# Moving the layernorms' normalized results from VectorE to ScalarE in a fused tokenizer, retention and MoE kernel

## The chip, the cores and the metric

The kernel runs on one NeuronCore of a Trainium2 chip. The metric is device time in microseconds (us) from the first to the last instruction of one execution; lower is better. The engines are called by their profile names: PE (TensorE matmul) and PEld (its weight load), DVE (VectorE), ACT (ScalarE), POOL (GpSimd) and SP (SyncE, which issues most of the DMA transfers). Each engine works through its own list of instructions, and semaphores join the lists.

## What is computed

The reference, cut to its steps, with D = 256 features, H = 1024, 8 experts, and 4 x 64 rows of 64 tokens (16,384 tokens):

```python
h = tok_ref(x, W)                          # patches -> rfft -> 256 features
# attention-like block on the layernorm of h
z  = layernorm(h)
zz = layernorm(z) * ln1_g + ln1_b
q, k, v = zz @ Wq.T + bq, zz @ Wk.T + bk, zz @ Wv.T + bv
mem_t = decay * mem_{t-1} + k_t * v_t ;  ret_t = q_t * mem_t
z  = z + ret
zz = layernorm(z) * ln2_g + ln2_b
h  = h + z + relu(zz @ W1.T + b1) @ W2.T + b2
# mixture of experts on the layernorm of h, the best 2 of 8 experts
tok = layernorm(h)
h   = h + tok + sum_over_2_experts(share_e * (gelu(tok @ w1[e] + b1[e]) @ w2[e] + b2[e]))
```

So each token passes four layernorms. The first two are one after the other (z, then zz from the same h: its factor is worked out directly from the variance of h), the third is zz after the retention, and the fourth is tok before the experts. Gains and offsets of the layernorms are folded into the weights; what is left of each is (x - mean) * rstd.

## The kernel before: the parts that matter

The tokens are worked on in 32 blocks of 512 (4 groups of 128 tokens, TT = 4). Three blocks are under way at a time: `new` is embedded and goes through retention, `mid` goes through the MLP, `old` is routed to the experts. Between them "slots" run expert tiles of 256 rows. The order on PE, DVE, ACT and SP is the order of the program text. Cuts are marked with `...`; line numbers of the profile (L252) are those of the whole kernel.

```python
    p_mm = ctx.enter_context(tc.tile_pool(name="p_mm", bufs=4, space=...PSUM))   # 4 buffers
    p_tm = ctx.enter_context(tc.tile_pool(name="p_tm", bufs=3, space=...PSUM))
    ...
        def factors(self, twice=False):            # on GpSimd: rstd = (var + eps) ^ -0.5
            ...
            nc.gpsimd.tensor_tensor(self.rstd, self.rstd, mhalf[:, 0:n, :], ALU.pow)    # L248

        def apply(self, dst, src, i=0):            # L252: (x - mean) * rstd, on DVE
            for t in range(TT):
                nc.vector.tensor_scalar(dst[:, t, :D], src[:, t, :], self.mv[:, t, 0:1],
                                        self.rstd[:, i, t : t + 1], ALU.subtract, ALU.mult)
    ...
    class Turn:                                    # a transpose of 32-bit data by DMA, as two 16-bit planes
        def split(self, src):                      # L278: two ACT copies  planes <- src
            ...
        def start(self, planes):                   # L286: SP issues DMA transposes  turned <- planes
            ...
        def join(self, dst, copy):                 # L292: four copies  dst <- turned
            ...
    def feature_mm(w, rhs, m):                     # L298
        ps = p_mm.tile([P, BLK], F32, name="mm")
        for k in range(KD):
            nc.tensor.matmul(ps, lhsT=w[:, k, ts(m, P)], rhs=rhs[:, k, :], ...)
        return ps
    ...
        def embed(self):
            ... # products of x on PE, sums on DVE, statistics of h on DVE
            norm.factors(twice=True)
            yield
            self.z = one.tile(...); self.zz = one.tile(...)
            norm.apply(self.zz, self.h, 1)
            norm.apply(self.z, self.h, 0)
        ...
        def residual(self):
            ... # ret transposed by PE (L451), z += ret (L454), statistics of z, on DVE
            norm.factors_here()                    # 12 small DVE instructions, L231 to L237
            self.zz = one.tile([P, TT, D], F32, name="zz")
            norm.apply(self.zz, self.z)
        ...
        def features2(self):                       # ACT copies hT <- turned
            self.turn.join(self.hT, nc.scalar.copy)

        def mlp_in(self, m):                       # m = 0..7
            ps = feature_mm(w1_sb, self.hT, m)
            nc.scalar.activation(self.aT[:, m, :], ps, AF.Relu, ...)                    # L482

        def mlp_out(self, u, ...):                 # L492 on PE, h += ps on DVE (L499), statistics
            ...
            if u == U - 1:
                self.norm.factors_here() if self.i >= NS - 1 else self.norm.factors()
                self.tok = one.tile([P, TT, D], F32, name="tok")
                self.norm.apply(self.tok, self.h)
                ...
                nc.vector.tensor_scalar(self.by[:, 0, :], rstd, 1.0, None, ALU.add)
                nc.vector.scalar_tensor_tensor(self.by[:, 1, :], mean, -1.0, rstd, ALU.mult, ALU.mult)

        def store(self):                           # L518: h = h * by0 + by1, four ACT instructions
            ...
            self.stored = nc.sync.dma_start(out=rows_of(self.i), in_=self.h)

        def rows(self):                            # L533: row <- tok, two ACT copies
            ...
    ...
    class Tile:                                    # 256 rows of one expert
        def turn(self):    ...                     # L792: xT <- xh, two ACT copies
        def enter(self):   ...                     # L799: ps = p_mm.tile(...), matmuls; L807: ge <- gelu(ps), ACT
        def leave(self):   ...                     # L816: ps = p_tm.tile(...), matmuls
        def sums(self):    ...                     # y on DVE, added to the output by an indirect DMA of GpSimd
    ...
            # one block of the loop
            embed = new.embed()
            next(embed)
            if mid: mid.features2()
            if old:
                old.rows()
                old.turn3()
                old.store()
            next(embed)
            next(embed)
            if mid: mid.sum_up()
            next(embed, None)
            slot(known)                            # an expert tile: turn of the next but one, enter, leave
            if old: old.join3()
            ...
            for m in range(KH):
                if mid: mid.mlp_in(m)
                if m == 1: new.split1()
                if m == TT - 1: slot(known)
                if m == KH - 3:
                    blocks[i + 1].differences(xs.pop(i + 1))
                    new.features1()
            ...     # logits of old, retention of new, slot, mid.mlp_out(0)
            new.residual()
            slot(known)
            ...
            new.split2()
            if mid: mid.mlp_out(1)
```

Of the kernel before, what the change touches and what calls it, by code (L numbers as in the profile page):

```python
# [12 lines left out]
F32 = mybir.dt.float32  # L13
# [6 lines left out]
P = 128  # L20
# [15 lines left out]
def vit_tower_kernel(  # L36
# [178 lines left out]
    class Norm:  # L215
# [23 lines left out]
        def factors(self, twice=False):  # L239
# [7 lines left out]
                )  # L247
            nc.gpsimd.tensor_tensor(self.rstd, self.rstd, mhalf[:, 0:n, :], ALU.pow)  # L248

        def apply(self, dst, src, i=0):  # L250
            for t in range(TT):
                nc.vector.tensor_scalar(  # L252
                    dst[:, t, :D],
                    src[:, t, :],
                    self.mv[:, t, 0:1],
                    self.rstd[:, i, t : t + 1],
                    ALU.subtract,
                    ALU.mult,
                )
# [49 lines left out]
    class Block:  # L309
# [32 lines left out]
        def embed(self):  # L342


            xv = self.xv.rearrange("p i (j w) n -> p i j (w n)", j=J)
            self.h = three.tile([P, TT, D], F32, name="h")
            h = [self.h[:, t, :] for t in range(TT)]

            def products(which):
                ps = p_tm.tile([P, 2, D], F32, name="tm")  # L350
                for n, i in enumerate(which):
                    for j in range(J):
                        nc.tensor.matmul(  # L353
                            ps[:, n, :], lhsT=xv[:, i, j, :], rhs=wu[:, i, j, :], start=j == 0, stop=j == J - 1
                        )
# [24 lines left out]
            norm.stats(self.h, TT - 1)  # L380
            norm.factors(twice=True)
            yield
            self.z = one.tile([P, TT, D], F32, name="z")
            self.zz = one.tile([P, TT, D], F32, name="zz")
            norm.apply(self.zz, self.h, 1)
            norm.apply(self.z, self.h, 0)

        def split1(self):
            if self.i < EARLY:
# [55 lines left out]
        def residual(self):  # L445
            norm = Norm()
            for u in range(U):
                ps = p_tm.tile([P, 2, D], F32, name="tm")
                for i in range(2):
                    for k in range(KD):  # L450
                        nc.tensor.transpose(  # L451
                            ps[:, i, ts(k, P)], self.ret[:, k, ts(2 * u + i, P)], ident
                        )
                nc.vector.tensor_tensor(self.z[:, ts(u, 2), :], ps, self.z[:, ts(u, 2), :], ALU.add)  # L454
                for i in range(2):
                    norm.stats(self.z, 2 * u + i)
            norm.factors_here()
            self.zz = one.tile([P, TT, D], F32, name="zz")
            norm.apply(self.zz, self.z)

        def sum_up(self):
            nc.vector.tensor_tensor(self.h, self.h, self.z, ALU.add)
# [2 lines left out]
        def split2(self):  # L465
            if self.i < EARLY:
                return
            self.turn = Turn()
            self.turn.split(self.zz)

# [13 lines left out]
        def mlp_out(self, u, between=None):  # L484
            if u == 0:
                self.norm = Norm()
            ps = p_tm.tile([P, 2, D], F32, name="tm")
            for i in range(2):
                if i and between:
                    between()  # L490
                for k in range(KH):
                    nc.tensor.matmul(  # L492
                        ps[:, i, :],
                        lhsT=self.aT[:, k, ts(u * 2 + i, P)],
                        rhs=w2_sb[:, k, :],
                        start=k == 0,
                        stop=k == KH - 1,
                    )
            nc.vector.tensor_tensor(self.h[:, ts(u, 2), :], ps, self.h[:, ts(u, 2), :], ALU.add)  # L499
            for i in range(2):  # L500
                self.norm.stats(self.h, u * 2 + i)
            if u == U - 1:
                self.norm.factors_here() if self.i >= NS - 1 else self.norm.factors()
                self.tok = one.tile([P, TT, D], F32, name="tok")
                self.norm.apply(self.tok, self.h)
                if self.i == NS:
                    nc.vector.tensor_tensor(self.h, self.h, self.tok, ALU.add)
                    return
                mean, rstd = self.norm.mv[:, :, 0], self.norm.rstd[:, 0, :]
                self.by = small.tile([P, 2, TT], F32, name="by")  # L510
                nc.vector.tensor_scalar(self.by[:, 0, :], rstd, 1.0, None, ALU.add)
                nc.vector.scalar_tensor_tensor(self.by[:, 1, :], mean, -1.0, rstd, ALU.mult, ALU.mult)

        def store(self):

            by = self.by
            for t in range(TT):
                nc.scalar.activation(  # L518
                    self.h[:, t, :],
                    self.h[:, t, :],  # L520
                    AF.Identity,
                    bias=by[:, 1, t : t + 1],
                    scale=by[:, 0, t : t + 1],
                )

            self.stored = nc.sync.dma_start(out=rows_of(self.i), in_=self.h)
# [1 line left out]

        def rows(self):

            self.row = two.tile([P, TT, RW], I32, name="row")
            for i, half in enumerate(halves(self.tok)):
                nc.scalar.copy(self.row.bitcast(U16)[:, :, i * D : (i + 1) * D], half)  # L533
# [415 lines left out]
    with tc.manual_schedule(engines=MANUAL):  # L949
        blocks[0].differences(xs.pop(0))  # L950
        xs[1] = load_x(1)
        for i in range(NS):
# [12 lines left out]
                old.turn3()  # L965
                old.store()
            next(embed)
            next(embed)
            if mid:
                mid.sum_up()  # L970
            next(embed, None)
            slot(known)
            if old:
                old.join3()
# [2 lines left out]
            for m in range(KH):  # L977
                if mid:
                    mid.mlp_in(m)
                if m == 1:  # L980
                    new.split1()
                if m == TT - 1:
                    slot(known)
                if m == KH - 3:
# [35 lines left out]
        old.turn3()  # L1020
        old.store()
        next(embed)
        next(embed)
        mid.sum_up()
        next(embed, None)
        expert_step()
        weights = load_bank()
        old.join3()
        for m in range(KH):
            mid.mlp_in(m)  # L1030
            if m in (1, 5):
                next(weights)
            if m == TT - 1:
# [150 lines left out]
```

## Time and profile before

| | before |
|---|---|
| time, median of 3 runs | 2202.25 us (2193.75 to 2203.81) |
| span of the profiled execution | 2216.1 us |
| PE busy | 2161.2 us, 98% |
| DVE busy | 1650.9 us, 74% |
| POOL busy | 873.1 us, 39% |
| ACT busy | 825.6 us, 37% |
| the four results of layernorms on DVE (L252), 128 instructions each | 44.8 + 44.2 + 44.2 + 44.0 us |

A row of the profile's groups names line, engine, operation, output <- inputs and shape; then the busy time and the mean of one in ns; then the idle time of the engine just before, and what ended it. A row of the timeline gives start and duration in us, and in brackets the idle time before it with its releaser. One matmul of the program text (32-bit) stands in the profile as two records, so one step `mlp_in(m)` is four records of 128x512.

### The profile page before, as it was taken

Reading aid. Unit: us, or ns where it says so; the run is one execution under the profiler, and the core shown is the slowest. Engines: PE = TensorE matmul, PEld = TensorE weight load, DVE = VectorE, ACT = ScalarE, POOL = GpSimd, SP = SyncE. Lnnn points to the kernel's source line nnn. Section 1 sums busy time; section 2 is a strip of 40 time slices with the busy share of each in tenths; the row PEclk is TensorE's granted clock in tenths of the full one; section 3 lists DMA queues with packets and bytes.
Section 4 is the critical chain, followed back from the end, with each engine's and each line's share of the span. In section 5 each row is a group of like instructions: output and inputs, shape, how many; then the busy total and the mean of one; then the engine's idle time right before and its main releaser. Section 6 shows DMA issues by size and latency. Waiting matters only on the chain.

```text
span 2216.1 us, 28920 instructions
## 1 busy us (share of the span) xinstructions
PE 2161.2 (98%) x8548; PEld 1544.3 (70%) x8548; DVE 1650.9 (74%) x5150; ACT 825.6 (37%) x1329; POOL 873.1 (39%) x760
## 2 busy tenths in 40 slices
PE   8999999999999999999999999999999999998999
PEld 6666666667676667777666777666677766676676
DVE  6678877778778777877877777777787777766454
ACT  1223323444334443432444432344443334442443
POOL 0022243344444434444434444443444444344444
PEclk9999999999999999999999999999999999999999
DMA  3022265676565677657567656665765666588743
GB/s 135 20 97 75 79 147 125 134 163 122 127 149 135 143 139 150 125 129 155 129 139 149 135 128 135 149 136 132 163 130 130 138 146 137 115 172 205 116 66 45
DMA packets 425389, 284.95 MB, mean 129 GB/s; under 512 B 355216, under 2 KB 391056, under 8 KB 421136
## 3 DMA queue, kind: packets, MB, share of 16 engines
q1 hardware_dynamic: 374304, 210.21, 41.4%
q0 software_dynamic: 49632, 67.39, 16.1%
q10 hardware_dynamic: 1296, 5.52, 1.0%
q8 instruction: 67, 1.10, 0.2%
q14 instruction: 90, 0.74, 0.1%
HBM read 118.36 MB, written 88.39 MB: 93 GB/s over the span
## 4 chain that ended last, share of the span: by engine, by line
PE 88%; DVE 3%; DMA 3%; ACT 3%; issue 2%; another core or an unknown queue 0%; POOL 0%; ACTq 0%; DVEq 0%; SPq 0%; POOLq 0%
PE mm L298 31%; PE tm L492 19%; PE tm L353 11%; PE mm L799 9%; PE tm L816 9%; DMA turned<-planes 3%; PE sm L557 2%; PE tm L888 1%; PE tm L451 1%; PE mm L871 1%; PE mm L131 1%; PE mm L265 1%; ACT h L518 1%; ACT row L533 1%; ACT hT L292 1%
## 5 line engine op out<-in xcount | busy, mean ns | idle before, releaser
L839 POOL DMA_INDIRECT out<-y,xg x262 | 429.3, 1638 | 501.0 <-DVE y L835 225.9
L492 PE MATMUL tm<-w_sb,aT 128*128 128x256 f32 x2048 | 462.3, 380 | 16.5 <-issue 14.6
L298 PE MATMUL mm<-hT,w_sb 128*128 128x512 f32 x1024 | 455.4, 596 | 10.7 <-ACT ge L807 5.7
L492 PEld LDWEIGHTS tm<-w_sb,aT 128*128 128x128 f32 x2048 | 387.2, 190 | 80.8 <-issue 27.1
L298 PEld LDWEIGHTS mm<-hT,w_sb 128*128 128x128 f32 x1024 | 193.9, 191 | 232.6 <-issue 207.6
L298 PE MATMUL mm<-hT,wqkv_sb 128*128 128x512 f32 x768 | 342.5, 602 | 4.2 <-DVE hT L292 4.2
L640 POOL DMA_INDIRECT xbuf<-row,to x248 | 242.3, 977 | 258.8 <-DVE full L699 182.4
L807 ACT ACTIVATE ge<-mm,w 128x256 f32<-128x256 f32 x262 | 109.3, 469 | 574.3 <-issue 525.8
L353 PE MATMUL tm<-wu,xv 128*128 128x256 f32 x1280 | 284.8, 381 | 0.0
L298 PEld LDWEIGHTS mm<-hT,wqkv_sb 128*128 128x128 f32 x768 | 145.3, 192 | 176.4 <-issue 160.4
L353 PEld LDWEIGHTS tm<-wu,xv 128*128 128x128 f32 x1280 | 244.3, 191 | 33.3
L799 PE MATMUL mm<-xT,w 128*128 128x256 f32 x1048 | 251.3, 383 | 1.5 <-DVE tile_share L828 1.5
L816 PE MATMUL tm<-w,ge 128*128 128x256 f32 x1048 | 247.6, 379 | 0.9 <-DVE y L833 0.9
L482 ACT ACTIVATE aT<-mm,vec 128x512 f32<-128x512 f32 x256 | 169.9, 684 | 173.7 <-PE mm L298 170.5
L799 PEld LDWEIGHTS mm<-xT,w 128*128 128x128 f32 x1048 | 195.6, 191 | 38.6 <-issue 13.1
L816 PEld LDWEIGHTS tm<-w,ge 128*128 128x128 f32 x1048 | 199.0, 190 | 31.3 <-issue 3.4
L792 ACT COPY xT<-xh 128x512 uint16<-128x512 uint16 x262 | 181.2, 761 | 5.4 <-DMA xh<-xbuf 5.3
L243 POOL TENSOR_SCALAR rstd<-mv 128x4 f32<-128x4 f32 x62 | 41.6, 671 | 319.2 <-DVE mv L224 317.3
L833 DVE TENSOR_TENSOR y<-tm,w 128x512 f32<-128x512 f32 x131 | 90.6, 692 | 70.5 <-PE tm L816 69.7
L416 ACT ACTIVATE ks<-mm,vec 128x512 f32<-128x512 f32 x64 | 44.0, 687 | 248.6 <-PE mm L298 248.6
L597 POOL TENSOR_TENSOR ex<-euler,second 128x4 f32<-128x4 f32 x32 | 34.7, 1084 | 247.1 <-DVE second L589 247.1
L418 DVE SCALAR_TENSOR_TENSOR kv<-mm,vec,ks 128x512 f32<-128x512 f32 x64 | 47.9, 748 | 108.9 <-PE mm L298 108.9
(155 smaller groups left out, 2498.2 us busy)
## 6 DMA issues: line engine op xcount, KB each, us to landing
w<-in_wex SPq DMA_DIRECT2D x113, 641.5 KB
xb<-in_x SPq DMA_DIRECT2D x32, 1040.0 KB
out<-h SPq DMA_DIRECT2D x31, 512.0 KB
bank<-in_wex ACTq DMA_DIRECT2D x8, 641.5 KB
out<-y,xg POOLq DMA_INDIRECT x262
xbuf<-row,to POOLq DMA_INDIRECT x248
xh<-xbuf SPq DMA_TRANSPOSE x131
xg<-xbuf SPq DMA_DIRECT2D x131, 4.0 KB
```

The lines of the kernel that those rows point to most:

```text
L298: nc.tensor.matmul(ps, lhsT=w[:, k, ts(m, P)], rhs=rhs[:, k, :], start=k == 0, stop=k == KD - 1)
L353: nc.tensor.matmul(ps[:, n, :], lhsT=xv[:, i, j, :], rhs=wu[:, i, j, :], start=j == 0, stop=j == J - 1)
L418: nc.vector.scalar_tensor_tensor(own_order(self.kv[:, m, :]), tiles_order(pv), vec[:, BV + m : BV + m + 1], own_order(ks), ALU.add, ALU.mult,)
L482: nc.scalar.activation(self.aT[:, m, :], ps, AF.Relu, bias=vec[:, MB1 + m : MB1 + m + 1])
L492: nc.tensor.matmul(ps[:, i, :], lhsT=self.aT[:, k, ts(u * 2 + i, P)], rhs=w2_sb[:, k, :], start=k == 0, stop=k == KH - 1,)
L640: write = nc.gpsimd.indirect_dma_start(out=xbuf, out_offset=bass.IndirectOffsetOnAxis(ap=to[:, c, t : t + 1], axis=0), in_=self.row[:, t, ...
L792: nc.scalar.copy(halves[:, :, :, 1 - i], self.xh[:, i * KD : (i + 1) * KD, :])
L799: nc.tensor.matmul(ps[:, m, :], lhsT=self.w[:, k * D + m * P : k * D + (m + 1) * P], rhs=self.xT[:, k, :], start=k == 0, stop=k == KD - 1,)
L807: nc.scalar.activation(self.ge[:, m, :], ps[:, m, :], AF.Gelu, bias=self.w[:, 5 * D + m : 5 * D + m + 1])
L816: nc.tensor.matmul(ps[:, c, :], lhsT=self.ge[:, k, ts(c, P)], rhs=w[:, (2 + k) * D : (3 + k) * D], start=k == 0, stop=k == KD - 1,)
L833: nc.vector.tensor_tensor(y, ps, w[:, 4 * D : 5 * D].unsqueeze(1).to_broadcast([P, 2, D]), ALU.add)
L839: add = nc.gpsimd.indirect_dma_start(out=out, out_offset=bass.IndirectOffsetOnAxis(ap=self.xg[:, c, NUMBER - D : NUMBER - D + 1], axis=0), ...
```

## The change

The results z, zz (twice) and tok are no longer made by DVE as (x - mean) * rstd. ACT makes them as x * rstd + less, with less = -mean * rstd worked out beforehand for all 512 tokens: by GpSimd right behind the factors where GpSimd makes these, by DVE where DVE makes them. The ACT instructions stand at places of ACT's order chosen for each result: zz of the first layernorms behind `mlp_in(0)`, z behind `mlp_in(2)`, zz of the third right ahead of its split into planes, tok at the head of `rows`. The aim is to take work and waits for GpSimd off DVE, the second busiest engine, and give it to ACT. The store takes its factor and offset from the same small tiles. For the last two blocks tok stays on DVE.

```diff
+        def offsets(self, engine, n=1):
+
+            self.less = small.tile([P, n, TT], F32, name=f"less{n}")
+            mean = self.mv[:, :, 0]
+            if engine is nc.vector:
+                engine.scalar_tensor_tensor(self.less[:, 0, :], mean, -1.0, self.rstd[:, 0, :], ALU.mult, ALU.mult)
+                return
+            nc.vector.tensor_scalar(mean, mean, -1.0, None, ALU.mult)
+            mean = mean.unsqueeze(1).to_broadcast([P, n, TT])
+            engine.tensor_tensor(self.less, mean, self.rstd, ALU.mult)
+
+        def apply_act(self, dst, src, i=0):
+            for t in range(TT):
+                nc.scalar.activation(
+                    dst[:, t, :D],
+                    src[:, t, :],
+                    AF.Identity,
+                    bias=self.less[:, i, t : t + 1],
+                    scale=self.rstd[:, i, t : t + 1],
+                )
 ...
             norm.factors(twice=True)
-            yield
-            self.z = one.tile([P, TT, D], F32, name="z")
-            self.zz = one.tile([P, TT, D], F32, name="zz")
-            norm.apply(self.zz, self.h, 1)
-            norm.apply(self.z, self.h, 0)
+            norm.offsets(nc.gpsimd, 2)
+            self.norm1 = norm
+
+        def result1(self, i):
+
+            if i:
+                self.zz = one.tile([P, TT, D], F32, name="zz")
+                self.norm1.apply_act(self.zz, self.h, 1)
+            else:
+                self.z = one.tile([P, TT, D], F32, name="z")
+                self.norm1.apply_act(self.z, self.h, 0)
 ...
             norm.factors_here()
+            norm.offsets(nc.vector)
+            self.norm2 = norm
+            if self.i < EARLY or self.i == NS:
+                self.result2()
+
+        def result2(self):
             self.zz = one.tile([P, TT, D], F32, name="zz")
-            norm.apply(self.zz, self.z)
+            self.norm2.apply_act(self.zz, self.z)
 ...
         def split2(self):
             if self.i < EARLY:
                 return
+            self.result2()
             self.turn = Turn()
             self.turn.split(self.zz)
 ...  # mlp_out
-                self.norm.factors_here() if self.i >= NS - 1 else self.norm.factors()
-                self.tok = one.tile([P, TT, D], F32, name="tok")
-                self.norm.apply(self.tok, self.h)
+                here = self.i >= NS - 1
+                engine = nc.vector if here else nc.gpsimd
+                self.norm.factors_here() if here else self.norm.factors()
+                if self.i < NS:
+                    self.norm.offsets(engine)
+                    self.more = small.tile([P, TT], F32, name="more")
+                    engine.tensor_scalar(self.more, self.norm.rstd[:, 0, :], 1.0, None, ALU.add)
+                if here:
+                    self.tok = one.tile([P, TT, D], F32, name="tok")
+                    self.norm.apply(self.tok, self.h)
 ...
         def rows(self):
 
+            if self.i < NS - 1:
+                self.tok = one.tile([P, TT, D], F32, name="tok")
+                self.norm.apply_act(self.tok, self.h)
             self.row = two.tile([P, TT, RW], I32, name="row")
 ...  # the loop
             next(embed)
-            next(embed)
+            next(embed, None)
             if mid:
                 mid.sum_up()
-            next(embed, None)
             slot(known)
 ...
             for m in range(KH):
                 if mid:
                     mid.mlp_in(m)
+                if m == 0:
+                    new.result1(1)
                 if m == 1:
                     new.split1()
+                if m == 2:
+                    new.result1(0)
```

More of the change, by code (lines that the diff above doesn't have):

```diff
@@ L502, in mlp_out @@
             if u == U - 1:
-                self.norm.factors_here() if self.i >= NS - 1 else self.norm.factors()
-                self.tok = one.tile([P, TT, D], F32, name="tok")
-                self.norm.apply(self.tok, self.h)
+                here = self.i >= NS - 1
[8 more added lines that the diff above has]
+                    self.norm.apply(self.tok, self.h)
                 if self.i == NS:
                     nc.vector.tensor_tensor(self.h, self.h, self.tok, ALU.add)
[L508 to L512, printed above, removed]
         def store(self):
-            by = self.by
             for t in range(TT):
@@ L521, in store @@
                     AF.Identity,
-                    bias=by[:, 1, t : t + 1],
-                    scale=by[:, 0, t : t + 1],
+                    bias=self.norm.less[:, 0, t : t + 1],
+                    scale=self.more[:, t : t + 1],
                 )
@@ L1022, in vit_tower_kernel @@
         next(embed)
-        next(embed)
+        next(embed, None)
         mid.sum_up()
-        next(embed, None)
         expert_step()
@@ L1030, in vit_tower_kernel @@
             mid.mlp_in(m)
+            if m in (0, 2):
+                last.result1(m == 0)
             if m in (1, 5):
```

## The prediction, made before the changed kernel had run

> **What bounds the kernel now.** I begin with the page's busy times, because the change moves work between engines, and ask whether the engine that is relieved carries the time.
>
> ```profile
> PE 2161.2 (98%) x8548; PEld 1544.3 (70%) x8548; DVE 1650.9 (74%) x5150; ACT 825.6 (37%) x1329; POOL 873.1 (39%) x760
> ...
> PE 88%; DVE 3%; DMA 3%; ACT 3%; issue 2%; another core or an unknown queue 0%; POOL 0%; ACTq 0%; DVEq 0%; SPq 0%; POOLq 0%
> ```
>
> The second line is the share of the engines in the chain that ended last. PE is idle for 2216.1 - 2161.2 = 55 us in all. However much DVE is relieved, no more than these 55 us (2.5%) can be won, and part of them are the start and the end. So I ask in the table of waits what PE's idle time waits for, and what DVE and ACT wait for.
>
> ```profile
> ACT hT L292 <- DMA turned<-planes: 107.8, 25, 6.0
> ...
> DVE tok L252 <- POOL rstd L248: 87.9, 30, 4.7
> ...
> DVE zz L252 <- POOL rstd L248: 59.4, 32, 2.4
> ...
> PE tm L492 <- issue: 14.6, 34, 1.0
> ...
> PE mm L298 <- ACT ge L807: 5.7, 7, 1.2
> ```
>
> DVE loses 147 us to GpSimd's factors, but no wait of PE on `tok`, `z` or `zz` of any size stands in the table except one 4.9 us wait on `tok` in the last stage, and that `tok` stays on DVE. The last line matters more: PE already waits for ACT, seven times. Where, the timelines of ACT and then of PE show (start, duration, what, idle time before):
>
> ```profile
> 1511.34 2.63 ACT L292 COPY hT<-turned 128x512 uint16<-128x512 uint16 x4 [5.98 <-DMA turned<-planes]
> 1513.85 1.98 ACT L533 COPY row<-tok 128x1024 uint16<-128x1024 uint16 x2
> 1515.73 2.07 ACT L518 ACTIVATE h<-h,by 128x256 f32<-128x256 f32 x4
> 1517.71 1.37 ACT L792 COPY xT<-xh 128x512 uint16<-128x512 uint16 x2
> 1518.95 0.81 ACT L807 ACTIVATE ge<-mm,w 128x256 f32<-128x256 f32 x2
> 1519.67 1.24 ACT L482 ACTIVATE aT<-mm,vec 128x512 f32<-128x512 f32 x2
> ```
>
> ```profile
> 1511.49 1.89 PE L816 MATMUL tm<-w,ge 128*128 128x256 f32 x8
> 1513.22 5.38 PE L298 MATMUL mm<-hT,w_sb 128*128 128x512 f32 x12
> 1519.82 1.98 PE L298 MATMUL mm<-hT,w_sb 128*128 128x512 f32 x4 [1.22 <-ACT ge L807]
> ```
>
> From 1511 to 1520 us ACT has no gap. PE takes one buffer of `p_mm` for the tile's enter and three for `mlp_in(0)` to `(2)` (12 records); `mlp_in(3)` needs the tile's buffer back, and it is back when ACT has made `ge`, behind hT, row, the store's four instructions and xT. PE restarts 0.06 us after the second `ge` ends (1519.76). I followed this edge in the timeline through the 25 blocks from the eighth on: in seven PE waits, in the other eighteen `ge` ends 0.05 to 1.6 us before PE needs it, 0.74 on the mean. ACT is 37% busy over the span, but at this place it has almost nothing to spare.
>
> [...] `ge`'s matmuls ended at 1511.6, and `ge` still stood behind five groups. So the place in ACT's order decides. [...] four L518 (the same form: Identity with scale and bias, 128x256) take 2.07 us, 0.52 each, and I use that. [...] This trace shows a half clock after shorter waits: a wait of 1.47 us for hT at 1272 is followed by
>
> ```profile
> 1272.29 12.23 PE L298 MATMUL mm<-hT,wqkv_sb 128*128 128x512 f32 x24 [1.47 <-DVE hT L292]
> ```
>
> where the chain elsewhere has 10.40 us for the same 24 matmuls: 1.8 us more. Waits of 1.0 to 1.2 us mostly went without it, as at 1519.8 above.
>
> **The change part by part.** *DVE.* L252 leaves with 504 of 512 instructions (the last two blocks' tok stays). Four take 1.38 us in the timeline, so 126 x 1.38 = 174 us of DVE's stream go, and most of the 147 us of waits for rstd; some 60 small instructions for the offsets come and 60 (the store's) go. DVE falls to about 1,480 us. None of it lay on PE's path, so it brings 0 to 5 us.
>
> *GpSimd.* One more small instruction behind each of 62 factors and `more` behind 30. From rstd's 0.23 to 1.7 us each I take 1 us: 90 us, at 39% busy. In the block above rstd of the embedding ends at 1517.1 and `less` would end at about 1518.7; ACT reaches the new zz at 1520.3 or later. No wait is expected.
>
> *ACT.* 504 x 0.52 = 262 us more: 826 to about 1,090 us, 49%. By place, with the changed program's order of ACT: hT, **tok**, row, store, xT, ge, aT0, **zz**, aT1, planes, aT2, **z**, aT3, xT, ge, aT4 to aT7.
>
> 1. tok stands between hT and `ge` and pushes `ge` back by 2.07 us. In the seven blocks that already wait, all of it is new wait of PE; in the other eighteen 2.07 - 0.74 = 1.33: 7 x 2.07 + 18 x 1.33 = 38 us.
> 2. zz and z follow while PE does `mlp_in(3)` (1.72 us), the slot's tile (3.45) and `mlp_in(4)` to `(7)`. Counted from the end of `ge` (G): aT0 G+0.6, zz 2.7, aT1 3.3, planes 5.2, aT2 5.8, z 7.8, aT3 8.4, xT and ge 10.5. PE needs aT0's buffer at G+1.7, aT1's at 5.2, aT2's at 6.9, aT3's at 8.6, the second ge's at 10.3. All just fit; at most 0.2 us a block is lost, which I leave in the range.
> 3. The third layernorm's zz goes ahead of its planes, behind a `ge` that ends later than DVE's factors. Its planes come 1.4 to 2.1 us later, 1.7 on the mean. But SP issues their transpose 1.1 to 3.3 us after they end today, since it first issues a tile's loads; of the 1.7 some 0.45 us remain on the mean. They delay hT, and with it everything ahead of `ge`: 25 x 0.45 = 11 us.
> 4. The waits at `mlp_in(3)` then last 1.3 to 3.5 us, 2.3 on the mean. That is above the 1.5 us after which the half clock came. Estimate: in 60% of 25 blocks a loss of 1.7 us, 25 us.
> 5. The planes of the first zz end at G+5.2, not G+3.0, but SP issues their transpose at G+6.7 today, behind the row's transposes, the store and the slot's loads, which all move with ACT. So hT of the retention moves with `ge`. The five waits of PE for it (4.2 us in all, two followed by the half clock) may vanish, as PE arrives later: -7 us.
> 6. In the last stage zz of the last block feeds PE transposes while PE is waiting anyway: +1 to 2 us.
>
> The early blocks have no `ge` in this place; there tok, row and store end just as `mlp_in(0)` does, and nothing is lost. Sum: 38 + 11 + 25 - 7 + 1 = +68 us, 2202 + 68 = 2270 us.
>
> **Rivals.** *DVE was the hidden limit.* Its 74% and its 147 us of waits for rstd speak for it, and DVE's transposed copies feed PE. Then the relief would shorten the 4.2 us wait for hT and the 14.6 us of "issue" waits in L492, which fall together with DVE's factor chain; the result would be 2180 to 2200 us. Against it: the hT waits end with a DMA, PE waits for DVE elsewhere by tenths, and the cap is 55 us.
>
> *Hidden anyway.* If ACT made up the 2.07 us (tok made during the 6 us in which ACT waits for `turned`), nothing would change: 2195 to 2215 us. The order speaks against it: tok stands behind hT's copies.
>
> *ACT becomes the bound of the whole stage.* From the landing of hT to aT7, ACT has about 25.5 us of work where PE has 22.5. If the z and zz waits don't just fit, or if the half clock follows each wait, each block loses 4 to 5 us: 2300 to 2325 us.
>
> *GpSimd blocks ACT.* `less` stands behind scatter DMAs of 1.6 us each; DVE's waits for rstd reached 4.7 us. Then ACT, not DVE, would stand still in front of tok or zz, and PE behind it: another 20 to 40 us. In the block shown GpSimd has the embedding's factors over a microsecond early, so I count it little.
>
> **Range and chances.** Point 1 alone, with no half clock, gives about 2235; points 1 to 4 in full with a half clock in every block about 2300. I predict 2268 us, 2232 to 2305 for 8 in 10. Faster by 2% needs 44 of PE's 55 idle us: 3%. Slower by 2% begins at 2246, which points 1 and 3 reach with a little of point 4: 77%. Within 2%: 20%.
>
> **What would show it.** In the changed profile: DVE near 1,480 us and ACT near 1,090 us; L252's successors at 0.52 us each on ACT; PE's busy time nearly the same or raised by the half clock, but a line "PE mm <- ACT ge" with some 25 waits and 40 to 60 us where it had 7 and 5.7; tok between hT and row in ACT's timeline without a gap; the half clock in many blocks. I would be wrong if PE's waits for `ge` do not grow, if the L492 waits vanish together with DVE's zz, or if ACT waits for `less`.

## The result, and the profile after

The changed kernel takes 2301.27 us (2300.29 to 2304.10) where the kernel before took 2203.03 us beside it: a ratio of 1.0453, 95% interval 1.0417 to 1.0489. It is slower by 4.5%, 98 us. The prediction was 2268 us (2232 to 2305).

In the changed kernel the line numbers have moved: L319 is the line of `feature_mm` (L298 before), L845 that of `ge` (L807), L313 the copies of `turned` (L292), L516 `aT` (L482), L837 and L854 the tile's matmuls (L799, L816). New are L263, the layernorms' results on ACT, and L259, `less` on GpSimd. First the busy times on the profile's page:

```profile
PE 2192.8 (95%) x8548; PEld 1556.7 (68%) x8548; DVE 1498.0 (65%) x4680; ACT 1069.8 (47%) x1833; POOL 904.6 (39%) x852
```

The work moved as intended: DVE lost 153 us and ACT gained 244. What counts is the first entry. PE has the same 8548 records, but its busy time rose from 2161.2 to 2192.8 us, and its idle time from 55 to 2300.4 - 2192.8 = 107.6 us. So two things grew: waits, and the duration of the same matmuls. The table of waits (in all, times, longest) names the first:

```profile
ACT hT L313 <- DMA turned<-planes: 134.2, 25, 6.2
...
PE mm L319 <- ACT ge L845: 68.9, 25, 3.3
ACT zz L263 <- POOL less L259: 24.2, 7, 6.1
...
PE mm L837 <- issue: 8.4, 1, 8.4
PE mm L319 <- ACT aT L516: 7.1, 4, 2.7
...
PE mm L286 <- ACT zz L263: 4.5, 1, 4.5
```

PE's wait for `ge`, seven times and 5.7 us in the profile that the prediction used, stands in all 25 blocks that have the slot in this place, 2.76 us on the mean. The wait for `hT` ahead of the retention, 4.2 us before, is gone from PE's list. ACT's timeline of one block, then PE's:

```profile
1440.16 2.63 ACT L313 COPY hT<-turned 128x512 uint16<-128x512 uint16 x4 [5.85 <-DMA turned<-planes]
1442.66 2.06 ACT L263 ACTIVATE tok<-h,less,rstd 128x256 f32<-128x256 f32 x4
1444.76 1.99 ACT L571 COPY row<-tok 128x1024 uint16<-128x1024 uint16 x2
1446.65 2.07 ACT L553 ACTIVATE h<-h,less,more 128x256 f32<-128x256 f32 x4
1448.63 1.36 ACT L830 COPY xT<-xh 128x512 uint16<-128x512 uint16 x2
1449.86 0.82 ACT L845 ACTIVATE ge<-mm,w 128x256 f32<-128x256 f32 x2
1450.58 0.68 ACT L516 ACTIVATE aT<-mm,vec 128x512 f32<-128x512 f32 x1
1451.15 2.07 ACT L263 ACTIVATE zz<-h,less,rstd 128x256 f32<-128x256 f32 x4
```

```profile
1442.16 5.31 PE L319 MATMUL mm<-hT,w_sb 128*128 128x512 f32 x12
1450.73 3.05 PE L319 MATMUL mm<-hT,w_sb 128*128 128x512 f32 x4 [3.26 <-ACT ge L845]
1453.58 2.56 PE L837 MATMUL mm<-xT,w 128*128 128x256 f32 x8
```

tok stands between hT and row without a gap, as predicted, and `ge` begins 9.7 us after the start of hT's copies where it began 7.6 us after it. PE restarts when the second `ge` ends (1450.68). The second row is also the other loss: four records that took 1.98 us in the kernel before take 3.05, and the eight after them 2.56, not 1.89; the granted clock is 0.64 and 0.72 over these two rows, where it was 1.00 over the four records of the kernel before. The mean granted clock of the whole run fell from 0.991 to 0.975.

### The profile page after: what moved, and what is told of

The parts are those of the page before. It is cut to its first block, busy times and chain, and to the rows that moved or that the text cites. A ratio compares the mean times of both kernels' runs of the same rounds, so it can differ in the third digit from the quotient of the medians.

```text
span 2300.4 us, 28990 instructions
## 1 busy us (share of the span) xinstructions
PE 2192.8 (95%) x8548; PEld 1556.7 (68%) x8548; DVE 1498.0 (65%) x4680; ACT 1069.8 (47%) x1833; POOL 904.6 (39%) x852
## 5 line engine op out<-in xcount | busy, mean ns | idle before, releaser
L319 PE MATMUL mm<-hT,w_sb 128*128 128x512 f32 x1024 | 490.7, 629 | 76.2 <-ACT ge L845 68.9
L526 PE MATMUL tm<-w_sb,aT 128*128 128x256 f32 x2048 | 454.5, 379 | 2.0 <-DVE h L533 1.6
L319 PEld LDWEIGHTS mm<-hT,w_sb 128*128 128x128 f32 x1024 | 198.9, 198 | 314.1 <-issue 194.3
L845 ACT ACTIVATE ge<-mm,w 128x256 f32<-128x256 f32 x262 | 109.2, 469 | 512.6 <-issue 373.5
L319 PE MATMUL mm<-hT,wqkv_sb 128*128 128x512 f32 x768 | 340.3, 599 | 1.1 <-ACT hT L287 1.1
L837 PE MATMUL mm<-xT,w 128*128 128x256 f32 x1048 | 261.5, 394 | 8.4 <-issue 8.4
L319 PEld LDWEIGHTS mm<-hT,wqkv_sb 128*128 128x128 f32 x768 | 144.6, 192 | 171.6 <-issue 155.9
L854 PE MATMUL tm<-w,ge 128*128 128x256 f32 x1048 | 248.2, 380 | 0.9 <-DVE y L871 0.9
L837 PEld LDWEIGHTS mm<-xT,w 128*128 128x128 f32 x1048 | 205.4, 200 | 58.4 <-issue 23.2
L854 PEld LDWEIGHTS tm<-w,ge 128*128 128x128 f32 x1048 | 199.8, 191 | 31.6 <-issue 4.7
L516 ACT ACTIVATE aT<-mm,vec 128x512 f32<-128x512 f32 x256 | 172.1, 684 | 72.7 <-PE mm L319 71.8
L313 DVE COPY tokT<-turned 128x512 uint16<-128x512 uint16 x120 | 44.1, 450 | 202.4 <-DMA turned<-row 202.4
```

The source lines that it names most:

```text
L516: nc.scalar.activation(self.aT[:, m, :], ps, AF.Relu, bias=vec[:, MB1 + m : MB1 + m + 1])
L526: nc.tensor.matmul(ps[:, i, :], lhsT=self.aT[:, k, ts(u * 2 + i, P)], rhs=w2_sb[:, k, :], start=k == 0, stop=k == KH - 1,)
L837: nc.tensor.matmul(ps[:, m, :], lhsT=self.w[:, k * D + m * P : k * D + (m + 1) * P], rhs=self.xT[:, k, :], start=k == 0, stop=k == KD - 1,)
L845: nc.scalar.activation(self.ge[:, m, :], ps[:, m, :], AF.Gelu, bias=self.w[:, 5 * D + m : 5 * D + m + 1])
L854: nc.tensor.matmul(ps[:, c, :], lhsT=self.ge[:, k, ts(c, P)], rhs=w[:, (2 + k) * D : (3 + k) * D], start=k == 0, stop=k == KD - 1,)
```

## The experiments

Two sums per run carry the comparison, both from the first part of the page: PE's idle time (span less busy) and PE's busy time, which grows mainly by slower matmuls, since their number is the same. Differences are against the second profile of the kernel before (shown under "The two profiles of the kernel before": busy 2154.1, idle 38.4).

| run | time, us | ratio to before, 95% | PE idle | PE busy |
|---|---|---|---|---|
| after | 2301.3 | 1.0453 (1.0417 to 1.0489) | +69.2 | +38.7 |
| tok back on DVE | 2211.4 | 1.0044 (1.0026 to 1.0062) | +14.9 | +6.6 |
| only tok on ACT | 2277.4 | 1.0344 (1.0310 to 1.0379) | +49.4 | +35.4 |
| tok ahead of hT | 2212.0 | 1.0051 (1.0025 to 1.0077) | +15.7 | +3.5 |
| tok, row, store ahead of hT | 2252.8 | 1.0241 (1.0213 to 1.0270) | +42.4 | +15.1 |
| ge ahead of xT | 2258.0 | 1.0269 (1.0235 to 1.0303) | +42.3 | +20.3 |
| first z, zz back on DVE | 2283.6 | 1.0371 (1.0318 to 1.0424) | +55.8 | +30.6 |
| third zz back on DVE | 2292.1 | 1.0423 (1.0385 to 1.0461) | +61.9 | +37.7 |
| before, store late | 2238.7 | 1.0187 (1.0148 to 1.0226) | +25.4 | +14.2 |
| before, tok ahead of hT, store late | 2247.4 | 1.0198 (1.0173 to 1.0223) | +30.5 | +37.2 |
| after, tok ahead of hT, store late | 2252.7 | 1.0212 (1.0185 to 1.0238) | +35.2 | +33.3 |
| before, store late, its DMA later still | 2197.3 | 0.9984 (0.9967 to 1.0001) | -1.1 | +10.2 |

The two sums belong to the one execution that was profiled, the time to the median of all. They differ most for the two runs with tok ahead of hT and the store late, whose profiled executions took 14.5 us (the kernel before) and 10 us (after) more than their medians; elsewhere the two lie within some 6 us.

The theory is that tok's place ahead of `ge` carries most of the loss, by pushing `ge` back and by the slow clock after the longer wait. The rivals: that ACT's added work carries it wherever it stands, and that the other moved results (z, zz, zz of the third layernorm) carry it.

### Tok back on DVE, and tok alone on ACT

The first run undoes one part of the change, the second does that part alone.

```diff
  # mlp_out of the changed kernel
+                self.tok = one.tile([P, TT, D], F32, name="tok")
+                self.norm.apply(self.tok, self.h)
  # rows
-            if self.i < NS - 1:
-                self.tok = one.tile([P, TT, D], F32, name="tok")
-                self.norm.apply_act(self.tok, self.h)
```

> The changed kernel with tok made by DVE again (126 - the rest of the change stays). Theory 'place': tok's four instructions ahead of ge are what PE waits for at mlp_in(3); without them the 68.9 us of waits for ge fall to about 15 us (what remains is the third layernorm's zz, which delays hT by some 0.5 us), the half clock leaves most blocks, and the time is 2205 to 2225 us. Rival 'load': ACT has too much work in the whole stage from hT to the last aT, wherever it stands; a third of the added ACT work goes, so a third of the loss: 2265 to 2275 us.

```diff
  # rows of the kernel before; mlp_out's own tok is left out for these blocks
+            if self.i < NS - 1:
+                self.tok = one.tile([P, TT, D], F32, name="tok")
+                for t in range(TT):
+                    nc.scalar.activation(self.tok[:, t, :], self.h[:, t, :], AF.Identity,
+                        bias=self.by[:, 1, t : t + 1], scale=self.norm.rstd[:, 0, t : t + 1])
```

> The kernel before with tok alone moved to ACT, at the head of rows; z and both zz stay on DVE. Theory 'place': this alone gives waits for ge of 45 to 55 us and the half clock in more than half of the blocks: 2265 to 2285 us. Rival 'load': a third of the loss, 2230 to 2240 us.

The waits of the first, then of the second:

```profile
PE mm L319 <- ACT ge L841: 12.4, 18, 1.2
PE mm L833 <- ACT xT L826: 8.4, 1, 8.4
PE mm L319 <- ACT aT L516: 7.3, 4, 2.6
```

```profile
PE mm L298 <- ACT ge L818: 65.6, 25, 3.3
```

With tok back, 2211.39 us: 90 of the 98 us are gone, although the other three results, 180 us of ACT's added 244, stay on ACT. With tok alone, 2277.43 us: 75 of the 98 us are there. The rival that any added work costs has fallen. What the first run still loses are mostly the two other waits of its fence (8.4 and 7.3 us), which return below.

### Tok where ACT stands still

The changed kernel, with ACT's order alone altered: tok ahead of hT's copies, in the time in which ACT waits for the transposed data.

```diff
 ...         # rows no longer makes tok; make_tok holds the same four instructions
+            if old:
+                old.make_tok()
             if mid:
                 mid.features2()
             if old:
                 old.rows()
```

> The changed kernel with tok's four ACT instructions ahead of the copies of hT (features2), where ACT stands still for 4 to 6 us for the transposed planes; the same work, another place. Theory 'place': tok falls into that idle time, the waits for ge fall to 10 to 20 us, 2205 to 2225 us. Rival 'load': nothing changes, 2290 to 2305 us. If ACT has to wait for GpSimd's factors of tok there, hT comes later and part of the loss stays.

```profile
ACT tok L263 <- POOL less L259: 57.0, 26, 2.8
...
ACT hT L313 <- DMA turned<-planes: 24.5, 22, 2.2
PE mm L319 <- ACT ge L848: 13.4, 16, 1.2
```

It took 2212.01 us, the same as with tok on DVE. ACT's wait for `turned` has fallen from 134.2 to 24.5 us, filled by tok and by tok's wait for `less`, and `ge` is as early as before. The instructions are the same; only their place differs, and it is worth 89 us. So it is the place, not the work.

Putting row and the store ahead of hT too was to take them off the way to `ge` as well:

```diff
+            if old:
+                old.rows()
+                old.store()
             if mid:
                 mid.features2()
             if old:
-                old.rows()
                 old.turn3()
-                old.store()
```

> The changed kernel with tok, row and the store's four instructions all ahead of the copies of hT; the DMA transposes of row stay behind. Theory 'place': 6.1 us of ACT work go into an idle time of 4 to 6 us, so hT comes up to 1 us later at most, but ge stands 4.1 us earlier than in the kernel before: no waits for ge, no half clock, and the waits of 16 us in the second product of the MLP that the changed kernel has lost stay away: 2170 to 2195 us, faster than both. Rival 'load': 2280 to 2305 us.

```profile
ACT tok L263 <- POOL less L259: 57.8, 26, 2.7
PE mm L319 <- ACT hT L313: 40.5, 25, 2.1
```

This missed: 2252.81 us. No wait for `ge` is left, but hT itself is late in all 25 blocks, 1.6 us on the mean. ACT's 6 us of waiting hold the wait for `less` (2.2 us on the mean) and tok's 2.1 us, not row's 2.0 and the store's 2.1 besides. The space was overrated.

### The clock after a wait

Here the tiles' `ge` stands ahead of the xT copies of a later tile, so that it comes about 1.2 us earlier, with all four results on ACT.

```diff
-        advance("turn", n + 2)
         advance("enter", n + 1)
+        advance("turn", n + 2)
```

> The changed kernel with one swap in the slots: ge ahead of the two copies xT of a later tile. The work is the same on every engine; ge stands 1.25 us earlier. Theory 'place, and a half clock above a wait of about 1.5 us': the 25 waits for ge fall from 2.8 to about 1.5 us each (31 us in all), and the half clock leaves half of the blocks or more (another 20 us): 2245 to 2262 us. Rival 'the half clock does not depend on the length of the wait': 2266 to 2272 us. Rival 'load': no change.

```profile
PE mm L319 <- ACT ge L845: 26.4, 22, 2.1
PE mm L319 <- ACT aT L516: 15.8, 28, 2.2
...
PE mm L837 <- ACT xT L830: 12.1, 9, 9.1
```

2257.95 us, as expected. The waits for `ge` fall by 42.5 us and the busy time of PE by 18.4 us. PE's idle time falls by 26.9 us only, since other waits grow: those for `aT` from 7.1 to 15.8 us, and some for xT and hT come up. What stood behind `ge` with just enough room no longer has it.

The profile also records when the granted clock was halved, mostly for 3.41 us or a multiple of it:

| profile | half-clock stretches | us in all | half of what was added | PE busy, added |
|---|---|---|---|---|
| before, second | 7 | 30 | | |
| after | 27 | 117 | 44 | 38.7 |
| ge ahead of xT | 10 | 50 | 10 | 20.3 |
| tok ahead of hT | 7 | 41 | 6 | 3.5 |

The third column of numbers is an estimate: the time that matmuls would lose to the added stretches if PE were busy throughout them. For the changed kernel it covers the growth of the busy time; for the run of this section it covers half, and the rest stays open.

Of all waits for `ge` in all profiles, none of the 78 under 1.5 us is followed by the half clock (a stretch that begins in the wait or within 3.5 us behind it), 2 of the 10 from 1.5 to 2 us, and 80 of the 94 from 2 us on. In the blocks shown such a wait cost 1.7 us more than itself (1.07 us in four records, 0.67 in the next eight). This is no rule of length alone: of PE's waits for the retention's `hT`, 17 of the 48 under 1 us and 13 of the 27 from 1 to 1.5 us are followed by the half clock too. In the run before, tok ahead of hT, store late, with 23 waits of 1.75 us there, 12 of the 25 stretches last 6.8 us, and the busy time grew by 37.2 us. Why that place is more sensitive was not tried.

### The other results

The first run undoes the first two layernorms' results, the second the third's.

```diff
  # embed, as in the kernel before
-            norm.offsets(nc.gpsimd, 2)
-            self.norm1 = norm
+            yield
+            self.z = one.tile([P, TT, D], F32, name="z")
+            self.zz = one.tile([P, TT, D], F32, name="zz")
+            norm.apply(self.zz, self.h, 1)
+            norm.apply(self.z, self.h, 0)
  # and the calls of result1 in the loop are gone
```

> The changed kernel with z and zz of the first two layernorms made by DVE again; tok and the third layernorm's zz stay on ACT. Theory 'place': z and zz stand behind ge and just fit between the MLP's activations, so the waits for ge stay at 60 to 70 us; only the early blocks, where ACT stands still for GpSimd's offsets, win 10 to 15 us: 2283 to 2293 us. Rival 'load' (half of the added ACT work goes): 2245 to 2260 us.

```diff
             norm.factors_here()
-            norm.offsets(nc.vector)
-            self.norm2 = norm
-            ...
             self.zz = one.tile([P, TT, D], F32, name="zz")
-            self.norm2.apply_act(self.zz, self.z)
+            norm.apply(self.zz, self.z)
```

> The changed kernel with the third layernorm's zz made by DVE again; tok, z and zz of the first two stay on ACT. Theory 'place': hT comes 0.3 to 0.6 us earlier, so the waits for ge fall by 8 to 15 us, and the 8.5 us wait of the last stage, where ACT stands in front of this zz, goes: 2275 to 2288 us. Rival 'load' (a quarter of the added work goes): 2270 to 2280 us. The two overlap; the waits for ge in the profile tell them apart.

The waits of the first, then of the second:

```profile
PE mm L319 <- ACT ge L848: 67.4, 25, 3.3
...
PE mm L840 <- ACT xT L833: 8.4, 1, 8.4
```

```profile
PE mm L319 <- ACT ge L838: 66.2, 25, 3.3
ACT zz L263 <- POOL less L259: 25.5, 7, 6.0
...
PE mm L319 <- ACT aT L509: 8.0, 4, 2.7
```

Without the first two results on ACT the kernel takes 2283.64 us, as expected, 18 us less than the changed one (the two intervals overlap a little), and PE's wait for `ge` is nearly untouched. What left the list are the waits for `aT` and the 4.5 us for zz. They lie in the early blocks, as the changed kernel's timeline shows, ACT first and then PE:

```profile
131.23 2.08 ACT L263 ACTIVATE zz<-h,less,rstd 128x256 f32<-128x256 f32 x4 [6.13 <-POOL less L259]
133.21 1.24 ACT L516 ACTIVATE aT<-mm,vec 128x512 f32<-128x512 f32 x2
```

```profile
133.93 3.68 PE L319 MATMUL mm<-hT,w_sb 128*128 128x512 f32 x4 [2.69 <-ACT aT L516]
```

ACT stands 6 us for GpSimd's `less`, `aT` stands behind zz, and PE waits 2.7 us and goes on at about half its pace (3.68 us for four records, against 1.98 at a granted clock of 1.00 in the kernel before; here it is 0.51). The wait for GpSimd that DVE used to bear now stands in ACT's order, ahead of something that PE needs.

The third layernorm's zz back on DVE brings 9 us, less than expected, with intervals that overlap; the `ge` waits fall by 2.7 us only. What does go is the 8.4 us wait of the last stage, which no longer stands in the list of this run (two others, of 1.8 and 1.7 us, do). Its timeline in the changed kernel, ACT and then PE:

```profile
2129.89 2.07 ACT L263 ACTIVATE zz<-z,less,rstd 128x256 f32<-128x256 f32 x4 [11.65 <-DVE rstd L237]
2131.87 1.36 ACT L830 COPY xT<-xh 128x512 uint16<-128x512 uint16 x2
```

```profile
2133.28 3.78 PE L837 MATMUL mm<-xT,w 128*128 128x256 f32 x8 [8.36 <-issue]
```

A tile's xT stands behind zz of the last block, and zz waits for DVE's factors: a tile that was free to run is held up by a result that it doesn't use.

### The two profiles of the kernel before

The prediction leaned on one profile of the kernel before. It was taken a second time, unchanged.

> The kernel before, unchanged, with a second profile. The first profile of it has 24 us of waits of PE inside the second product of the MLP (L492), which stand in none of the profiles since; that of the kernel with only tok moved has 0.3 us there, though its code at that place is the same. If these waits belong to the kernel before and the change takes them away, they stand in this profile again (15 to 25 us). If they belong to that one profiled execution, they are under 3 us here, the span is near 2200 us, and the change takes nothing away there.

```profile
PE 2154.1 (98%) x8548; PEld 1545.9 (71%) x8548; DVE 1652.9 (75%) x5150; ACT 825.7 (38%) x1329; POOL 877.2 (40%) x760
```

```profile
PE mm L298 <- ACT ge L807: 14.4, 19, 1.2
...
PE mm L298 <- DVE hT L292: 3.4, 6, 1.3
```

The span is 2192.5 us, not 2216.1. The 14.6 us of "issue" waits at L492 are absent (the expectation's 24 us are these and 9.9 at two other lines), and 19 of the 25 blocks wait for `ge`, not seven. A likely reason, only argued here, is that a PE undelayed elsewhere comes to `mlp_in(3)` earlier, and less time is left for `ge`. This is the better base for what tok costs: 65.6 - 14.4 = 51 us of waits, 2.05 us in each of 25 blocks, which is tok's duration.

### What stands next to the limit

If `ge` is late in 19 blocks of the kernel before, it could gain by moving something off its way. The store (2.07 us of ACT, and a DMA of 512 KB) can go behind it. Three runs: the kernel before with that alone, the kernel before with tok on ACT ahead of hT as well, and the changed kernel with both moves.

```diff
             if old:
                 old.rows()
                 old.turn3()
-                old.store()
 ...
             slot(known)
             if old:
+                old.store()
                 old.join3()
```

> The kernel before, with nothing of the change, but with the store (four ACT instructions, 2.07 us, and its DMA) behind the slot's `ge` instead of ahead of it. Place theory: `ge` ends 2.07 us earlier in each block, PE's 14.4 us of waits for `ge` fall to under 3 us, and SP issues the slot's loads a little earlier; 2180 to 2195 us, 0.3 to 0.9% under the kernel before. Rival (each place of ACT is equally tight): the store in front of aT0 makes PE wait for aT instead, some 10 us of such waits, and the time stays within 0.2% of before or above it.

> The kernel before with only tok given to ACT, at the place ahead of hT's copies, and the store behind the slot's `ge`; z and both zz stay on DVE. Place theory: ACT has the 6 us wait for the transposed data there, so tok costs nothing, and the time is that of the run with only the store moved, within 0.2%: 2180 to 2195 us. If giving tok away relieves DVE in a way that PE feels: 5 us or more under that run. If tok in front of hT delays hT: waits of PE for hT of over 10 us and a time above the kernel before.

> The changed kernel with tok ahead of hT's copies (as before in the run with tok early) and the store behind the slot's `ge`. Place theory: the 13.4 us of waits for `ge` that were left there go, the 8.4 us of the last stage and the early blocks' 8 to 12 us for `less` stay; 2197 to 2208 us, within 0.3% of before. If DVE's relief (some 170 us of its stream) is worth something by itself: under 2192 us. If z and zz behind `ge` collide with the store that now follows it: waits of PE for aT of over 10 us, and 2215 us or more.

All three missed on the slow side. The signs named for tok in front of hT (waits for hT, a time above before) and for a collision of z and zz with the store (waits for aT of over 10 us) did appear, but the first run, which moves neither tok nor z and zz, has 36.3 us of waits for the retention's hT too. The waits of each, in the order of the expectations:

```profile
PE mm L298 <- DVE hT L292: 36.3, 24, 2.7
```

```profile
PE mm L298 <- DVE hT L292: 40.2, 23, 3.0
...
ACT hT L292 <- DMA turned<-planes: 29.4, 23, 2.6
```

```profile
PE mm L319 <- DVE hT L313: 30.3, 20, 3.0
...
PE mm L319 <- ACT aT L516: 10.6, 12, 2.5
```

The waits for `ge` at `mlp_in(3)` are gone in all three, but the wait for `hT` of the retention, 3.4 us before, has taken their place. SP's queue in one block shows what had moved, first in the kernel before (second profile), then with the store late:

```profile
1443.44 0.52 SPq L526 DMA_DIRECT2D out<-h  x1
...
1449.43 2.82 SPq L286 DMA_TRANSPOSE turned<-planes  x1
```

```profile
1473.13 0.40 SPq L526 DMA_DIRECT2D out<-h  x1
1473.75 4.93 SPq L286 DMA_TRANSPOSE turned<-planes  x1
```

The transposes of the first zz used to start 5.3 us or more behind the store's DMA, and now mostly 0.6 us behind it. The row of these transposes lasts 3.53 us (median of 25 blocks) in the first and 4.71 in the second. To tell whether the transfer does that, or PE's earlier arrival, the last run moves only the DMA behind the transposes:

```diff
                 if m == 1:
                     new.split1()
+                    if old:
+                        old.store_out()      # the store's DMA; its ACT part stays behind the slot
```

> As the run with the store moved behind the slot's `ge`, but the store's DMA (512 KB) is issued behind the DMA transposes of the first zz instead of 0.6 us ahead of them. If those transposes were late because the store's transfer ran beside them: PE's 36.3 us of waits for the retention's hT fall to under 10 us, the waits for `ge` stay under 3 us, and the time is 2180 to 2200 us, the kernel before or up to 0.9% under it. If they were late for another reason (SP's queue, or PE simply arriving earlier, since it no longer waits for `ge`): the waits for hT stay above 20 us and the time above 2220 us.

```profile
PE mm L298 <- DVE hT L292: 15.1, 17, 2.1
```

```profile
1456.72 3.37 SPq L286 DMA_TRANSPOSE turned<-planes  x1
1460.15 0.57 SPq L528 DMA_DIRECT2D out<-h  x1
```

The time falls from 2238.67 to 2197.25 us by the place of one DMA, and the transposes' row has a median of 3.62 us again. From the end of the planes to the first copy of hT 9.85 us pass (median of 25), where 10.73 passed with the store ahead: 22 us in 25 blocks, about what the waits for hT fell by (21.2). So the store's place ahead of the transposes was the larger part. Moving it takes two things away at once, though, its transfer beside the transposes and its 0.6 us ahead of them in SP's queue: the row begins 0.66 us earlier behind the planes and lasts 1.1 us less. The two were not tried apart. The rest, 15.1 us where under 10 were expected, has room for the other reason: PE no longer waits for `ge`, so it reaches the retention up to 1.2 us earlier and meets hT there. That part was not tried by itself. The net gain over the kernel before is 0.16%, and the interval touches 1: it beats the changed kernel by 104 us, but not the kernel before.

These runs also bear on what DVE's relief is worth. Tok given away at a place that is free (second run of the three against the first) takes 34 us of DVE's busy time, and the ratio is 1.0198 against 1.0187: no gain shows, though the intervals would hide one of up to some 10 us. The run with tok ahead of hT has DVE at 1499.0 us, 154 less than before, and is 0.5% slower than before.

## Why the prediction was right, and where it was not

The direction, the place and the range held: tok ahead of `ge`, PE waiting in all 25 blocks, DVE at 1498 and ACT at 1070 us, the slow clock. The time lies only 4 us inside the upper end, and it is also the lower end of a rival, that ACT becomes the bound of the whole stage (2300 to 2325 us). Half of that rival's condition came true, the half clock behind most waits; the other half did not: z and zz make PE wait in none of the 25 blocks, and ACT stands still there for 5.9 us. The sum of +68 us was too small by some 30; between the second profile of before and the profile of after it is +107.9, of which 69.2 are PE's idle time and 38.7 slower matmuls. The largest shortfalls are the half clock (14 us), the early blocks' waits for `aT` and zz (12) and the last stage (7).

Two of the three signs of being wrong appeared: ACT waits for `less` (24.2 us), and the waits at L492 are down to 0.3 us. The first is a miss, below. The second is not the change's doing, since they are absent from the second profile of the kernel before too.

- **Point 1, tok pushes `ge` back by 2.07 us: right, size off.** The term was 38 us and measured 51. The mechanism held, 2.05 us a block, but "the other eighteen" blocks with 0.74 us to spare came from a profile in which PE was delayed elsewhere. In the second profile 19 blocks already wait, and nearly the whole 2.07 us counts everywhere. (At 1511.6 us, `ge` stood behind four groups, not five.)
- **Point 2, z and zz "just fit": right for the middle blocks.** The four waits for `aT` of the changed kernel all lie in early blocks; in the other 25, with zz and z in place, PE doesn't wait for `aT`. The run with `ge` ahead of xT, where xT then stands ahead of `aT`, shows how little room is left: 28 waits for `aT`, 15.8 us.
- **Point 3, the third zz delays hT, 11 us: hardly there.** Taking it back lowers the waits for `ge` by 2.7 us. The step had the delay of the planes too long and what SP absorbs too small. With this zz on ACT the planes end 1.2 us later on the mean of 25 blocks (1.7 predicted), SP issues their transposes 1.68 us behind them instead of 2.63, and hT starts 0.13 us later (0.45 predicted).
- **Point 4, half clock in 60% of blocks, 25 us: right, size off.** 38.7 us, since the waits are 2.76 us on the mean and not 2.3, and 21 of the 25 are followed by it, not 60%; at 1.7 us each these are 36 us. (The 1.8 us of the prediction compares a row of the timeline with one of the chain; a row of 24 undisturbed matmuls takes 10.55 us, so the loss was 1.7; the granted clock is 1.00 over that row and 0.86 over the prediction's of 12.23 us.) Most waits for `ge` from 2.0 to 3.3 us have the half clock behind them (80 of 94 in all profiles). Of the 27 stretches of the changed kernel 22 last 3.41 us, and all begin whole multiples of 3.41 us apart.
- **Point 5, the waits for hT of retention vanish: right**, 3.4 us (4.2 in the first profile) and none after. The last section shows the other side: make `ge` earlier and they come back.
- **Point 6, the last stage, +1 to 2 us: wrong in size.** 8.4 us. The step looked at PE's transposes of zz, and not at xT of a tile that stands behind zz in ACT's order.
- **"Nothing is lost" in the early blocks, and "No wait is expected" for `less`: wrong.** In the block shown GpSimd starts the factors only at 125.5 us, released by DVE's `mv`, when ACT is done with `aT` of `mlp_in(0)` (125.1), and needs until 131.2 us for them and `less`, so ACT stands 6 us. Taking these results back brought 18 us. The rival that GpSimd blocks ACT, of which the prediction said "I count it little", was right for these blocks at about its lower figure, though not for its reason: in the block shown no scatter DMA stands ahead of `less`. GpSimd's added work was 31 us, not 90.
- **DVE relief, 0 to 5 us: not contradicted.** Nothing shows, but the intervals are wider than 5 us.

## What to carry to other kernels

Work given to an engine with 60% idle time costs by its place in that engine's order: the same four instructions cost nothing in front of a wait for data (2212.0 us, against 2211.4 with tok on DVE) and some 75 to 90 us behind it. The timelines shown give the reason: ACT's instructions ran in the order of the program, and `ge`, whose matmuls ended at 1440.6 us, began at 1449.86, behind hT, tok, row, the store and xT. So before moving work, list what stands behind the new place, what the moved work itself waits for, and how much each has to spare, in more than one profile. In this kernel, whose PE was 98% busy, several such margins were of a microsecond or so (0.74 us on the mean in eighteen blocks at `ge`), and clearing one mostly uncovered the next: with the store behind `ge` its 14.4 us of waits went, and those for the retention's `hT` grew from 3.4 to 36.3 us.

## What the runs showed that was not expected

Waits of PE for `ge` of 2 to 3 us cost more than themselves: 25 waits of 2.76 us came with 38.7 us of slower matmuls, more than half again, while none of the 78 waits for `ge` under 1.5 us had the half clock behind it; at the retention shorter waits had it too. A 512 KB store issued 0.6 us ahead of DMA transposes came with a row of 4.71 us instead of 3.53, and cost 41 us of kernel time against the same store issued behind them. And two profiles of one unchanged kernel differed by 14.6 us of PE waits in a single line; in the first, eighteen blocks had 0.74 us to spare at `ge` on the mean, in the second 19 of 25 waited there.
